# MLP's second layer: where in the first outer product VectorE begins the operand sums of the second one

## The chip, the cores and the metric

One core of a Trainium2 chip runs one program. The time is the device time of one execution in microseconds (us); before the change it is 2250.13 us, the median of three runs (2246.69, 2250.13, 2252.49). The core has five engines that run side by side and meet in semaphores: TensorE (PE for matmuls, PEld for loads of weights), VectorE (DVE), ScalarE (ACT), GpSimd (POOL) and SyncE (SP, which here issues most DMAs).

## The reference

One transformer block on x of 2 x 2048 x 512, all in float32. A condition vector gives shifts, scales and gates:

```python
mod = silu(condition) @ Wada + bada
sh_a, sc_a, gt_a, sh_m, sc_m, gt_m = split(mod, 6, axis=1)
xm = layernorm(x, g1, be1) * (1 + sc_a) + sh_a
x = x + gt_a * attention(xm, Wqkv, Wproj, bproj)     # 16 heads, causal
xm = layernorm(x, g2, be2) * (1 + sc_m) + sh_m
h = gelu(xm @ W1 + b1)                               # 512 -> 2048
x = x + gt_m * (h @ W2 + b2)                         # 2048 -> 512
```

The change lies in `h @ W2`.

## The kernel before

The kernel runs its stages one after the other: modulation, normalised and transposed x, queries, keys and values, attention with its projection (to about 1518 us), and then the MLP in four blocks (`m` = 0 to 3) of 1024 tokens each.

**Products of seven.** Large matrix products are split in two along each side and made with seven block products instead of eight, by Winograd's form of Strassen's method: products named A11, S1, S2, S4, S3, A12, A22, whose operands are blocks of the tokens, or sums and differences of such blocks, against blocks or sums of blocks of the weights. The MLP does this at two levels: seven **outer products**, each made of seven **inner products**. The sums for the weights are made early and kept in DRAM; the sums for the tokens are made by VectorE and GpSimd as the work runs.

**The first layer** of a block (`pair_of_sets`, L2205, for blocks 1 to 3; `first_pair` and `pair`, with single-level weights from the start, for block 0) leaves the hidden values h in eight tiles, gelu included. In the last of its steps for blocks 1 to 3 the gelu of four h tiles isn't issued there but put in the list `ends` (four ScalarE activations), which the second layer works off. For block 0 `ends` stays empty.

**The second layer** of a block is `tail` (L2353). It runs the outer products in the order A11, S1, A12, S2, S3, A22, S4. Each is one call of `outer` (L2284), which has `seven` (L1739) make seven inner products, each of four matmuls (four blocks of 128 of the inner side; a record counts eight, as float32 goes in two passes) of 128 x 256 into a PSUM bank. The inner order is A11, S1, S2, S4, S3, A12, A22, called products 1 to 7 here, or k = 0 to 6 in the code. The banks: products 1, 3, 5 and 7 go to bank ps_a, 2 and 4 to ps_b, 6 to ps_c. Products 3, 4, 5 and 7 add onto what their bank holds, after what it held has been copied out. That is a **drain**: `first` (L2322) behind products 1, 2, 3 and `last` (L2330) behind 4, 5, 6, 7. Where a drain adds (`combine`, L1734) it is on VectorE, where it only copies (L2325, L2335) on ScalarE. In the outer products A11 and S1 the drains behind products 1, 2, 3 and 7 are ScalarE copies, those behind 4, 5 and 6 VectorE additions; in A12, S2, S3, A22 all are VectorE's. Behind S2 and S3 stands one larger VectorE addition of 128 x 1024 each, between results in y.

**The sums.** An outer product needs differences of blocks of h: four for its inner products S1, S2, S3, A22 (`inner_sum`, L1924), and where its own operand is a difference (S1's T1, S2's T2, S3's T3, A22's T4), four pieces of that first. All are `difference` (L1637), of 128 x 1024, on VectorE but for a few early ones on GpSimd. They stand in one list `todo` in a fixed order:

```
A11: 1 | T1(0,0) T1(0,1) | S1: 1 | A11: 2 3 4 | T1(1,0) T1(1,1) | S1: 2 3 4 | A12: 1-4 |
T2 x4 | T1 done | S2: 1-4 | T3 x4 | S3: 1-4 | T4 x4 | A22: 1-4 | S4: 1-4
```

Sum 1 of an outer product is read by its inner product S1, sum 2 by S2, sum 3 by S3, sum 4 by A22. T1(1,1) is also an operand of S1's second sum. "T1 done" issues nothing and gives T1's buffers back. `pop` (L1934) takes the first item of the list and issues it, if a buffer is free (`sums`, a queue of tiles: the buffer given back first is taken first). `need` (L1944) pops until a given sum is issued; `outer` calls it ahead of each inner product for what that reads (and ahead of S1 for sum 2, ahead of S2 for sum 4). In blocks 1 to 3 the last step of the first layer has popped the list's first four items, and then calls for A11: 2, 3, 4.

**The order of the work.** `act` (L209) and `mm` (L205) keep instructions in the order in which the program calls them, engine by engine. So what `then(k)` (L2377) of `tail` issues behind inner product k stands on VectorE's queue behind that product's drain and ahead of the next product's. It issues, in this order: a gate on ScalarE where one is due; one item of `ends`, if there is any, but in A11 only from k = 4 on; one `hid.pop()`, under the condition that the change edits; and `among`, the normalisation and transposes (ps_xt, L215) of the next block's tokens behind k = 3 and 6 of the first four outer products, and its token sums in the last one. The transposes stand on TensorE between outer products. A weight tile's next load (`next_weights`, L1686) is issued behind the inner products S4 and A22.

GpSimd meanwhile adds products of the first layer onto h (L2228), ahead of the gelus in `ends`.

Of the kernel before, what the change touches and what calls it, by code (L numbers as in the profile page):

```python
# [27 lines left out]
def dit_block_kernel(  # L28
# [862 lines left out]
    S1, S2, A11, S4, A12, A22, S3 = range(7)  # L891
# [708 lines left out]
    with ExitStack() as mlp:  # L1600
# [132 lines left out]
        def combine(dst, x, y):  # L1733
            act(nc.vector.tensor_tensor(dst, x, y, ALU.add))  # L1734
# [609 lines left out]
        def gated(m, y, half, i, tok=slice(0, MT)):  # L2344
            b, k = m * 2 * MT // T, half * HK + i
            act(
                nc.scalar.activation(
                    y[:, i, tok], y[:, i, tok], AF.Identity,
                    bias=gbias[:, k, b : b + 1], scale=gb[:, k, b : b + 1],
                )  # L2350
            )

        def tail(m, hid, among, each):  # L2353

            u, c22, c11, c12 = Y
            later = []

            def gate(y, half):
                later.extend(lambda i=i: gated(m, y, half, i) for i in range(2))

            for n, dst, base in (
                (A11, u, None),
                (S1, c22, None),
                (A12, c11, u),  # L2370
                (S2, u, u),
                (S3, u, u),
                (A22, u, u),
                (S4, c12, c12),
            ):

                def then(k):  # L2377
                    if k in (1, 3) and later:
                        later.pop(0)()
                    if hid.ends and (n != A11 or k >= 4):  # L2380
                        hid.ends.pop(0)()
                    if n != A11 or k > 1 or not hid.ends:
                        hid.pop()
                    among(n, k)

                hid.outer(n, dst, base, then, each if n == S4 else None)
                if n == A12:
                    gate(c11, 0)
                elif n == S2:
                    combine(c12, u, c22)  # L2390
                elif n == S3:
                    combine(c22, c22, u)
                    gate(c22, 1)
                elif n == A22:
                    gate(u, 1)
                elif n == S4 and not each:
                    gate(c12, 0)
            for f in later:
                f()
# [31 lines left out]
        for m in range(NM):  # L2431
            hid = Hidden()
# [4 lines left out]
            for p in range(HF // 2):  # L2437

                def among(ph, r):
                    if p == HF // 2 - 1 and not ready:  # L2440
                        if (ph or r == 3) and len(hid.made) < 4:
                            hid.pop()
                    elif p == HF // 2 - 1:
                        if (ph, r) in ((1, 3), (2, 0), (2, 2), (2, 4)):
                            hid.pop()
                    if ready and p < 2 and ph and r in (1, 4):
                        rows_out(m - 1, p, res, [(0, C)], True, (2 * ph - 2 + r // 4,))
# [89 lines left out]
```

## Time and profile before

| | us |
|---|---|
| median of three runs | 2250.13 |
| lowest, highest | 2246.69, 2252.49 |
| profiled execution, its own time | 2247.25 |
| its span, first to last instruction | 2245.5 |
| TensorE busy | 2197.9 (98% of the span) |
| VectorE busy | 1578.2 (70%) |
| ScalarE busy | 1038.3 (46%) |
| GpSimd busy | 1456.7 (65%) |
| granted TensorE clock, mean | 0.997 |
| tails of blocks 1, 2, 3 begin at | 1782.89, 1963.99, 2144.98 |

How to read it: a row of a timeline has the start in us, the duration, the engine, the line of the kernel, the operation, what is written and read (buffer numbers left out), the shapes and the count of instructions that were merged; in brackets stands the idle time of the engine just before, and who ended it. A row of the waits has the waiting engine, tile and line, what it waited for, and the total, the number and the longest of such waits. Matmul ends are modelled, so distances between starts say more than durations. L207 is the helper of all matmuls, L1734 of all VectorE additions (`combine`), L1637 of the sums of blocks; the tile tells them apart: `sum` is a token sum, `y` and `c` are drains of the second layer, `ps_a`, `ps_b`, `ps_c` its banks.

### The profile page before, as it was taken

What the parts mean: (1) busy time and instruction counts of PE and PEld (TensorE: products, weight loads), DVE (VectorE), ACT (ScalarE), POOL (GpSimd) and SP (SyncE); (2) the same over time, 40 slices, a digit from 0 to 9 for tenths busy, and PEclk for the clock granted to TensorE, in tenths of its full rate; (3) what the DMA queues carried; (4) which work ended last, traced back from release to release, by engine and by line L of the source; (5) the groups of instructions that cost most, each with busy time, mean ns of one, the idle gap of its engine ahead of it and who ended that gap; (6) DMA issues with size and microseconds to landing.
All of it is one profiled execution on the core that took longest, in us unless ns stands there. A gap on an engine that the chain in (4) does not pass through costs nothing.

```text
span 2245.5 us, 34306 instructions
## 1 busy us (share of the span) xinstructions
PE 2197.9 (98%) x12273; PEld 1473.3 (66%) x12273; DVE 1578.2 (70%) x3373; ACT 1038.3 (46%) x2132; POOL 1456.7 (65%) x903
## 2 busy tenths in 40 slices
PE   7999999999999999999999999999999999999998
PEld 5787555555543588755555555345788888888887
DVE  4678767777757657777677766665687687687586
ACT  4434555655564243365655556614323523532520
POOL 4254988998983795299989898447416715625540
PEclk9999999999999999999999999999999999999999
DMA  8887142231324899532324113367655555554553
GB/s 280 249 276 191 44 91 67 62 86 48 108 96 139 261 299 314 156 80 71 77 69 102 48 49 131 106 232 260 209 173 207 173 160 169 202 169 157 195 161 107
DMA packets 166628, 340.99 MB, mean 152 GB/s; under 512 B 17217, under 2 KB 49517, under 8 KB 164665
## 3 DMA queue, kind: packets, MB, share of 16 engines
q1 hardware_dynamic: 158080, 302.05, 44.3%
q0 software_dynamic: 8000, 36.21, 4.3%
q8 instruction: 97, 1.59, 0.3%
q14 instruction: 75, 0.61, 0.1%
q10 hardware_dynamic: 376, 0.55, 0.1%
HBM read 246.46 MB, written 100.14 MB: 154 GB/s over the span
## 4 chain that ended last, share of the span: by engine, by line
PE 86%; DVE 6%; POOL 3%; DMA 2%; ACT 1%; issue 1%; SPq 0%; ACTq 0%; DVEq 0%; POOLq 0%
PE ps_a L207 22%; PE st L207 19%; PE ps_b L207 13%; PE o L207 10%; PE s L207 9%; PE ps_o L207 4%; PE ps_c L207 3%; PE sm L207 3%; DVE sum L1637 2%; DVE junk L503 1%; POOL ee L700 1%; PE ps_xt L215 1%; ACT e L675 1%; DVE mx L509 1%; PE ps_o L215 1%
## 5 line engine op out<-in xcount | busy, mean ns | idle before, releaser
L675 ACT ACTIVATE e<-st 128x512 f32<-128x512 f32 (+1 forms) x1152 | 574.9, 578 | 362.4 <-PE st L207 315.6
L509 DVE TENSOR_REDUCE mx<-s 128x1 f32<-128x512 f32 x576 | 381.7, 686 | 193.4 <-PE s L207 192.3
L700 POOL TENSOR_TENSOR ee<-ee,e 128x2048 f32<-128x2048 f32 x106 | 485.8, 4583 | 10.3 <-ACT e L675 4.3
L207 PE MATMUL st<-qst,kst 128*128 128x512 f32 (+3 forms) x1280 | 408.6, 386 | 0.0
L207 PE MATMUL s<-kst,qst 128*128 128x512 f32 (+3 forms) x1046 | 380.6, 395 | 5.7 <-DVE mx L509 3.7
L207 PE MATMUL ps_a<-sum,w 128*128 128x256 f32 (+1 forms) x1304 | 340.2, 395 | 8.3 <-DVE y L1734 7.7
L207 PE MATMUL o<-e,vv 128*32 128x512 f32 (+3 forms) x2560 | 293.2, 537 | 0.3
L207 PEld LDWEIGHTS st<-qst,kst 128*128 128x128 f32 x1280 | 228.5, 188 | 97.7 <-issue 66.0
L207 PEld LDWEIGHTS ps_a<-sum,w 128*128 128x128 f32 x1304 | 249.2, 193 | 51.5 <-DVE y L1734 8.9
L503 DVE CUSTOM_DVE_ANT_0 junk<-s,causal 128x128 bf16<-128x128 f32 (+3 forms) x470 | 220.7, 470 | 60.9 <-PE s L207 47.1
L207 PEld LDWEIGHTS s<-kst,qst 128*128 128x128 f32 x1046 | 194.8, 188 | 70.7 <-DVE mx L509 17.0
L700 POOL TENSOR_TENSOR ee<-e 128x2048 f32<-128x2048 f32 x42 | 192.5, 4584 | 42.7 <-ACT e L675 41.8
L207 PE MATMUL ps_b<-sum,w 128*128 128x256 f32 (+1 forms) x744 | 186.5, 381 | 0.0
L2228 POOL TENSOR_TENSOR h<-h,h 128x512 f32<-128x512 f32 x96 | 119.3, 1271 | 69.8 <-DVE h L1734 69.8
L207 PEld LDWEIGHTS <-sel 32*128 32x128 bf16 x1152 | 29.5, 91 | 197.0 <-issue 195.3
L207 PEld LDWEIGHTS ps_b<-sum,w 128*128 128x128 f32 x744 | 140.6, 190 | 21.8 <-issue 2.6
L509 DVE TENSOR_REDUCE mx<-st 128x1 f32<-128x512 f32 x192 | 131.1, 683 | 0.5
L1799 POOL TENSOR_TENSOR sum<-xm 128x256 f32<-128x256 f32 x22 | 23.2, 1053 | 162.6 <-PE ps_a L207 162.6
L687 POOL TENSOR_SCALAR_AFFINE_SELECT e<-e 128x512 f32<-128x512 f32 x128 | 83.2, 668 | 67.5 <-ACT e L675 67.4
L207 PEld LDWEIGHTS o<-e,vv 128*32 128x32 f32 x2560 | 59.1, 108 | 92.2 <-issue 73.4
L207 PE MATMUL st<-fold,sel 32*128 32x512 bf16 (+1 forms) x1152 | 117.5, 372 | 1.3
L1071 POOL TENSOR_TENSOR lo<-lo,hi 128x512 fp32r<-128x512 f32 x32 | 40.7, 1275 | 105.4 <-ACT hi L1069 103.5
(263 smaller groups left out, 3573.2 us busy)
## 6 DMA issues: line engine op xcount, KB each, us to landing
w<-w1x SPq DMA_DIRECT2D x42, 896.0 KB
qst<-q SPq DMA_DIRECT2D x128, 256.0 KB
kst<-k SPq DMA_DIRECT2D x128, 256.0 KB
w<-w2d SPq DMA_DIRECT2D x28, 1024.0 KB
w<-w2d SPq DMA_DIRECT2D x28, 768.0 KB
q<-hi SPq DMA_DIRECT2D x32, 256.0 KB
q<-lo SPq DMA_DIRECT2D x32, 256.0 KB
k<-hi SPq DMA_DIRECT2D x32, 256.0 KB
```

The lines of the kernel that those rows point to most:

```text
L207: return tc.keep_in_program_order(nc.tensor.matmul(*args, **kw))
L215: return tc.keep_in_program_order(nc.tensor.transpose(dst, src, ident[:n, :n]))
L503: nc.vector.tensor_tensor_reduce(junk[:, :w], x, causal[:, QB - w :], 1.0, MASKED, ALU.add, ALU.max, m,)
L509: self.vector(nc.vector.tensor_reduce(m, x, axis=AX.X, op=ALU.max))
L675: act(nc.scalar.activation(e4[:, h, :w], sts[h][:, :w], AF.Exp))
L687: nc.gpsimd.affine_select(d, d, pattern=[[0, HC], [1, P]], compare_op=ALU.is_ge, fill=0.0, base=0, channel_multiplier=-1,)
L700: act(nc.gpsimd.tensor_tensor(dst, x, y, ALU.add))
L1071: engine.tensor_tensor(lo, d, hi.bitcast(F32), ALU.subtract)
L1637: act(engine.tensor_tensor(dst, x, y, ALU.subtract))
L1799: act(engine.tensor_tensor(dst, u, v, ALU.subtract))
L2228: act(engine.tensor_tensor(d[j], d[j], x[j], ALU.add))
```

## The change

One number in the condition under which `then` pops a sum. In A11 of a block with a filled list `ends` (blocks 1, 2, 3), the pops behind k = 2 and k = 3 go; those behind k = 4, 5 and 6 stay. The list is worked off in the same order, so from T1(1,0) on each pop of it stands two inner products later.

```diff
                 def then(k):
                     if k in (1, 3) and later:
                         later.pop(0)()
                     if hid.ends and (n != A11 or k >= 4):
                         hid.ends.pop(0)()
-                    if n != A11 or k > 1 or not hid.ends:
+                    if n != A11 or k >= 4 or not hid.ends:
                         hid.pop()
                     among(n, k)
```

The order of VectorE's instructions in A11 and the start of S1 (block 1; drains named by their bank):

```
before: A11 2, A11 3, A11 4, T1(1,0), drain ps_b, T1(1,1), drain ps_a, S1 2, drain ps_c, S1 3, S1 4, A12 1, A12 2, A12 3, drain ps_b, A12 4
after:  A11 2, A11 3, A11 4, drain ps_b, drain ps_a, T1(1,0), drain ps_c, T1(1,1), S1 2, S1 3, S1 4, A12 1, drain ps_b, A12 2
```

In A22 the order after is: first drain, A22 2, second drain, A22 3, A22 4, third drain, S4 1; before it was: first drain, A22 4, second drain, S4 1, third drain, S4 2. TensorE, ScalarE and GpSimd have the same operations in the same order; which of the buffers of `sums` they use differs.

## The prediction

> **What bounds the kernel now.** I read the page's first part, then the waits of TensorE alone from 1500 us on (the MLP), then the timelines of TensorE and VectorE around each wait found there, and last the table of stretches for the clock.
>
> ```profile
> PE 2197.9 (98%) x12273; PEld 1473.3 (66%) x12273; DVE 1578.2 (70%) x3373; ACT 1038.3 (46%) x2132; POOL 1456.7 (65%) x903
> ```
>
> TensorE is the bound: 98% busy. A change that moves only VectorE work is worth what TensorE waits for VectorE, no more. The waits of TensorE from 1500 us to the end (total, times, longest):
>
> ```profile
> PE ps_a L207 <- DVE y L1734: 7.7, 3, 2.6
> PE ps_o L215 <- ACT y L2347: 1.5, 1, 1.5
> ...
> PE ps_a L207 <- DVE c L1734: 0.6, 3, 0.2
> ```
>
> The first row is three waits of about 2.6 us for a drain of bank ps_a into y. They stand in the first outer product (A11) of the tails of blocks 1, 2 and 3. The first block's tail has no such wait; its list `ends` is empty, so the edited condition is true there before and after, and nothing changes in it. Here is the second tail on TensorE:
>
> ```profile
> 1789.80 1.89 PE L207 MATMUL ps_a<-sum,w 128*128 128x256 f32 x8
> 1791.53 1.89 PE L207 MATMUL ps_c<-h,w 128*128 128x256 f32 x8
> 1796.00 3.55 PE L207 MATMUL ps_a<-sum,w 128*128 128x256 f32 x8 [2.58 <-DVE y L1734]
> 1799.38 1.04 PE L215 MATMUL ps_xt<-ident,xn 128*128 128x128 f32 x8
> 1800.26 1.89 PE L207 MATMUL ps_a<-sum,w 128*128 128x256 f32 x8
> ```
>
> The rows are inner products 5, 6, 7 of A11, the transposes, and product 1 of the next outer product (S1). Products start 1.73 us apart (1789.80 to 1791.53), transposes take 0.88. Product 7 could start at 1791.53 + 1.73 = 1793.26 and starts at 1796.00: **2.74 us**. It then takes 1799.38 - 1796.00 = 3.38 instead of 1.73: **1.65 us** more. VectorE at that time:
>
> ```profile
> 1785.61 3.37 DVE L1637 TENSOR_TENSOR sum<-h,h 128x1024 f32<-128x1024 f32 x1
> 1788.90 2.30 DVE L1637 TENSOR_TENSOR sum<-h,sum 128x1024 f32<-128x1024 f32 x1
> 1791.12 2.29 DVE L1637 TENSOR_TENSOR sum<-h,h 128x1024 f32<-128x1024 f32 x1
> 1793.33 0.41 DVE L1734 TENSOR_TENSOR y<-c,ps_b 128x256 f32<-128x256 f32 x1
> 1793.67 1.95 DVE L1637 TENSOR_TENSOR sum<-h,h 128x1024 f32<-128x1024 f32 x1
> 1795.54 0.41 DVE L1734 TENSOR_TENSOR y<-c,ps_a 128x256 f32<-128x256 f32 x1
> 1795.87 1.95 DVE L1637 TENSOR_TENSOR sum<-sum,sum 128x1024 f32<-128x1024 f32 x1
> 1797.74 0.41 DVE L1734 TENSOR_TENSOR y<-c,ps_c 128x256 f32<-128x256 f32 x1
> 1798.08 2.35 DVE L1637 TENSOR_TENSOR sum<-sum,sum 128x1024 f32<-128x1024 f32 x2
> ...
> 1851.78 1.22 DVE L1637 TENSOR_TENSOR sum<-h,h 128x1024 f32<-128x1024 f32 x1
> 1852.91 1.75 DVE L1734 TENSOR_TENSOR y<-y,y 128x1024 f32<-128x1024 f32 x1
> 1854.58 0.41 DVE L1734 TENSOR_TENSOR c<-y,ps_a 128x256 f32<-128x256 f32 x1
> 1854.91 1.21 DVE L1637 TENSOR_TENSOR sum<-h,sum 128x1024 f32<-128x1024 f32 x1
> ```
>
> Rows 1 and 2 are the last two of three sums that A11 itself needs; rows 3 and 5 (1791.12, 1793.67) are T1(1,0) and T1(1,1), for the second outer product. The drain of product 5 (1795.54) ends at 1795.95 and product 7 starts at 1796.00. Product 5 had been ready at 1789.80 + 1.89 = 1791.69: the drain was late because two T1 sums stood before it.
>
> Why product 7 is slow is seen in the table of stretches (columns: the stretch, its length, busy time and instructions of PE, PEld, DVE, ACT, POOL, then the granted clock of TensorE, the DMA share, GB/s):
>
> ```profile
> 1793.30:1796.00 2.70, 0.12 (x1) 0.00 (x1) 2.70 (x5) 0.00 (x0) 2.70 (x2) 0.96 0.98 370
> 1796.00:1799.40 3.40, 3.40 (x9) 2.70 (x10) 3.40 (x4) 0.00 (x0) 0.74 (x1) 0.53 0.05 20
> 1799.40:1802.80 3.40, 3.40 (x21) 3.12 (x20) 3.30 (x3) 3.21 (x8) 0.00 (x0) 1.00 0.48 133
> 1977.10:1980.40 3.30, 3.30 (x9) 2.66 (x10) 3.30 (x4) 0.00 (x0) 0.72 (x1) 0.55 0.03 10
> 2158.10:2161.40 3.30, 3.30 (x9) 2.72 (x10) 3.30 (x4) 0.00 (x0) 0.72 (x1) 0.56 0.00 0
> ```
>
> After each wait the clock is 0.53, 0.55, 0.56 for some 3.3 us; after the first of them it is seen back at 1.00. That loses 3.40 x 0.47 = 1.60 in the second tail (1.65 by the starts), 3.30 x 0.45 = 1.49 in the third and 3.30 x 0.44 = 1.45 in the last.
>
> **The change, part by part.** No instruction is added or removed on any engine. Only `hid.pop()` of A11 behind products 3 and 4 goes, in three tails: every VectorE sum from T1(1,0) on stands two places later among the drains, and their buffers rotate accordingly. No DMA and no POOL instruction is moved past another.
>
> *Saved, at A11's product 7.* Behind the sum that ends at 1791.20 now stand two drains: product 4's (ps_b, ready long before), done by about 1791.5, then product 5's, which waits for 1791.69, starts near 1791.73 and ends by 1792.14. Product 7 can go at 1793.26 with 1.1 us to spare. The wait goes whole, 2.74 us in each tail (three alike by the waits row), 8.2 in all. With no idle time, I take it that the clock stays 1.00: 1.65 + 1.49 + 1.45 = 4.6. **Saved 12.8 us**.
>
> *What is late next: S1's product 3.* It needs S1's second sum, which needs T1(1,1). S1 now starts at 1793.26 + 1.73 + 0.88 = 1795.87, so product 3 is due 3.46 later, at 1799.33. GpSimd slows the sums for as long as its own additions last:
>
> ```profile
> 1787.86 8.88 POOL L2228 TENSOR_TENSOR h<-h,y 128x512 f32<-128x512 f32 x4
> ```
>
> They end at 1796.74. VectorE: T1(1,0) from 1792.07 at a pitch of 2.21 (1788.90 to 1791.12) to 1794.28; product 6's drain, 0.34; T1(1,1) at most 2.21 more, to 1796.83; the S1 sum, now free of GpSimd, 1.22, to 1798.05 (1798.8 at the 1.95 of its row). It is 0.5 to 1.3 us early; cost nothing. S1's third and fourth sums follow at about 1.2 each (2.35 for two in the row), ready by 1801.2, before products 5 and 7, due 6.9 and 10.4 after 1795.87. Bank ps_c, which S1 takes over for its second product, is drained by 1794.7, before 1797.6. The cover here is these 0.5 us; past it each microsecond of lateness costs one.
>
> *Then.* In S1's later half, A12, S2 and S3 VectorE has one sum and one drain per product, 1.22 + 0.42 = 1.64 under 1.73; the queue has the same slots, each with a sum of two places before. The task "T1 done" issues nothing and takes one pop wherever it falls. Each sum of S2 and S3 still stands ahead of the product that reads it by a product or more: nothing.
>
> *Lost, at A22 (sixth outer product).* Here there was no spare. Slots by the last four VectorE rows above: a sum (1851.78), the large addition into y (1852.91), a drain, a sum (1854.91). Now the slot at 1851.78 holds A22's first sum and that at 1854.91 its second. TensorE before:
>
> ```profile
> 1852.96 1.89 PE L207 MATMUL ps_b<-sum,w 128*128 128x256 f32 x8
> 1855.05 1.99 PE L207 MATMUL ps_a<-sum,w 128*128 128x256 f32 x8 [0.20 <-DVE c L1734]
> ```
>
> Product 2 reads the first sum, done at 1853.00: 0.1 late at most, which the next wait swallows. Product 3 reads the second, done at 1854.91 + 1.21 = 1856.12, so starts at 1856.17 instead of 1855.05: **1.12 us**. Behind it VectorE has to issue A22's third and fourth sums in one place (product 3 calls for the fourth), one 1.13 us pitch more, ahead of product 3's drain; but that drain's data is 1.12 later too, so nothing more comes late. Same in the third tail. In the last one, where the large addition is shorter:
>
> ```profile
> 2213.13 1.89 PE L207 MATMUL ps_a<-sum,w 128*128 128x256 f32 x8
> ```
> ```profile
> 2212.82 1.22 DVE L1637 TENSOR_TENSOR sum<-h,sum 128x1024 f32<-128x1024 f32 x1
> ```
>
> 2212.82 + 1.22 + 0.05 = 2214.09, less 2213.13: 0.96. **Lost 3.2 us** if the clock stays. The idle time there is about 1.4 us. The nearest row for that is the ps_o wait of the list of waits:
>
> ```profile
> 2230.69 0.77 PE L215 MATMUL ps_o<-ident,y 128*128 128x128 f32 x5 [1.52 <-ACT y L2347]
> ```
> ```profile
> 2230.70:2233.00 2.30, 2.30 (x13) 2.06 (x14) 1.29 (x2) 0.00 (x0) 0.00 (x0) 1.00 0.18 67
> ```
>
> 1.52 us idle, and 1.00 after it. Bounds for the clock at A22: nothing, or 1.6 us a tail as after the 2.58 us waits; 1.4 lies by the 1.52 row, so I take nothing.
>
> **Sum**: 12.8 - 3.2 = 9.6 us. The profiled execution took 2247.25 us (span 2245.5): 2237.7. The three runs have their median at 2250.13, 2.9 above it: **2240.5 us**. About 0.3% (6.75 us) is what a measurement of this kernel can tell from no change.
>
> *A rule against it.* The Trainium skill, TensorE: Matmul & The Clock Gate, section "HAM oscillation — how this bites in real kernels", wants idle gaps of more than about 3.4 us before TensorE falls back to half clock. The rows above show 0.53 behind an idle time of 2.58, so the trace does not bear that threshold out. If the clock there is low for a reason other than the wait, 1.6 us a tail stay: the third rival.
>
> **The rivals.**
> 1. *The A22 wait costs clock too* (1.4 us idle is enough): 3 x 1.6 = 4.8 back, 4.8 saved, 2245.3. For it: 2.58 is not far off and there is one row at 1.52. Against: that row. Chance 0.12.
> 2. *A22 costs nothing* (its sums come earlier than the slots say): 12.8 saved, 2237.3. Against: VectorE has no idle time in that stretch. 0.07.
> 3. *The low clock stays without the wait*: 8.2 - 3.2 = 5.0 saved, 2245.1. Against: 1.00 wherever TensorE runs through. 0.05.
> 4. *Slower: the wait moves to S1's product 3.* If the three sums T1(1,0), T1(1,1) and S1's second each take the longest of their kind, 3.37 (the row at 1785.61, beside a larger GpSimd operation): 1792.07 + 3.29 + 0.34 + 3.29 + 3.37 = 1802.4 against 1799.33, 3.1 idle, 1.6 of clock behind it, 1.1 at A22, less 4.3 saved: +1.5 a tail, 2254.6; with the clock lost at A22 too, +9.3, 2259.4. It decides from 1799.33 + 4.3 - 1.1 - 1.6 = 1800.9 on. Against: GpSimd's additions end at 1796.74. 0.07.
> 5. *It doesn't do what it says*: product 5's drain is held by something other than the sums. Against: VectorE runs without a gap from 1788.90 to it. 0.03, 2250.
>
> **How the numbers follow.** The forecast has 0.66. It lies 2.9 us beyond the bound of 6.75; the runs of before lie up to 3.4 from their median, so I give 0.06 of it to "within". Faster: 0.60 + 0.07 = 0.67. Within: 0.06 + 0.12 + 0.05 + 0.03, and half of rival 4: 0.29. Slower: 0.04. The range takes in the forecast and rivals 1, 2 and 3, 2237.3 to 2245.3, and about a microsecond of scatter: 2236 to 2246.
>
> **What would show it.** Right: the 7.7 us row of TensorE waiting for DVE y is gone; no stretch near 0.5 of the clock in the MLP; S1's first product starts 5 products and 0.88 us after A11's third; a new row of TensorE waiting for a sum (L1637), three times, 1.2 to 1.4 us, before A22's third product, with the clock 1.00 behind it. Wrong: a wait before S1's third product, or a low clock at A22. If both are absent and the gain is not near 9.6, one of the lengths above does not hold.

## The result, and the profile after

The changed kernel takes 2239.77 us in the median of five runs (2239.39 to 2241.53), beside 2246.96 for five runs of the kernel before (2245.70 to 2252.49). The ratio is 0.9963, with a 95% interval of 0.9948 to 0.9978: faster by 8.3 us, between 4.9 and 11.7. The two medians themselves lie 7.2 apart. The forecast was 2240.5, a ratio of 0.9957, 9.6 us less. The profiled execution took 2239.77 us, its span is 2238.1.

The same lines as before, now of the changed kernel. First the page's part 1, then TensorE's waits from 1500 us on:

```profile
PE 2195.8 (98%) x12273; PEld 1470.5 (66%) x12273; DVE 1581.7 (71%) x3373; ACT 1038.3 (46%) x2132; POOL 1456.9 (65%) x903
```
```profile
PE ps_a L207 <- DVE sum L1637: 2.9, 3, 1.1
PE ps_o L215 <- ACT y L2347: 1.5, 1, 1.5
PE ps_o L215 <- DVE xr L1734: 1.1, 3, 0.5
PE ps_a L207 <- DVE c L1734: 0.2, 1, 0.2
```

The three waits of 2.6 us for a drain into y are gone; three waits of up to 1.1 us for a sum have come. The counts of instructions are the same. In the busy shares nothing is to be seen of either: a wait of 8 us in 2240 is below a per cent.

TensorE in the tail of block 1, products 5, 6 and 7 of A11, the transposes, and the first three products of S1:

```profile
1791.98 1.89 PE L207 MATMUL ps_a<-sum,w 128*128 128x256 f32 x8
1793.71 1.89 PE L207 MATMUL ps_c<-h,w 128*128 128x256 f32 x8
1795.44 1.89 PE L207 MATMUL ps_a<-sum,w 128*128 128x256 f32 x8
1797.16 1.04 PE L215 MATMUL ps_xt<-ident,xn 128*128 128x128 f32 x8
1798.04 1.89 PE L207 MATMUL ps_a<-sum,w 128*128 128x256 f32 x8
1799.77 1.89 PE L207 MATMUL ps_b<-sum,w 128*128 128x256 f32 x8
1801.49 1.89 PE L207 MATMUL ps_a<-sum,w 128*128 128x256 f32 x8
```

The products start 1.73 us apart, and the transposes take 0.88. VectorE beside it:

```profile
1791.08 2.29 DVE L1637 TENSOR_TENSOR sum<-h,sum 128x1024 f32<-128x1024 f32 x1
1793.30 0.41 DVE L1734 TENSOR_TENSOR y<-c,ps_b 128x256 f32<-128x256 f32 x1
1793.91 0.42 DVE L1734 TENSOR_TENSOR y<-c,ps_a 128x256 f32<-128x256 f32 x1 [0.20 <-PE ps_a L207]
1794.25 1.34 DVE L1637 TENSOR_TENSOR sum<-h,h 128x1024 f32<-128x1024 f32 x1
1795.64 0.42 DVE L1734 TENSOR_TENSOR y<-c,ps_c 128x256 f32<-128x256 f32 x1
1795.98 1.83 DVE L1637 TENSOR_TENSOR sum<-h,h 128x1024 f32<-128x1024 f32 x1
1797.91 4.38 DVE L1637 TENSOR_TENSOR sum<-sum,sum 128x1024 f32<-128x1024 f32 x3
```

Both drains now stand ahead of the T1 sums; the second even waits 0.20 us for TensorE, so VectorE is ahead here and no longer behind. The granted clock there is 1.00 (columns as in the prediction; it is the third from the right):

```profile
1795.40:1798.80 3.40, 3.40 (x21) 3.04 (x21) 3.25 (x4) 1.44 (x4) 3.40 (x2) 1.00 0.75 281
1854.00:1857.40 3.40, 3.40 (x16) 3.01 (x17) 3.40 (x5) 0.00 (x0) 0.00 (x0) 1.00 0.00 0
```

The second of these rows lies behind the new wait, at A22's third product. That wait on TensorE, and the sum it waits for on VectorE:

```profile
1849.01 1.89 PE L207 MATMUL ps_a<-h,w 128*128 128x256 f32 x8
1850.83 1.99 PE L207 MATMUL ps_b<-sum,w 128*128 128x256 f32 x8
1853.96 1.99 PE L207 MATMUL ps_a<-sum,w 128*128 128x256 f32 x8 [1.14 <-DVE sum L1637]
```
```profile
1850.69 1.75 DVE L1734 TENSOR_TENSOR y<-y,y 128x1024 f32<-128x1024 f32 x1
1852.36 0.41 DVE L1734 TENSOR_TENSOR c<-y,ps_a 128x256 f32<-128x256 f32 x1
1852.69 1.21 DVE L1637 TENSOR_TENSOR sum<-h,sum 128x1024 f32<-128x1024 f32 x1
```

The best measure in one execution is the length of a tail, from A11's first matmul to S4's first, since what comes before the MLP moves it little or not at all. Of the kernel before: 80.90, 80.79, 76.79 us in blocks 1, 2, 3 (starts 1782.89 to 1863.79, 1963.99 to 2044.78, 2144.98 to 2221.77). Of the changed one: 77.61, 77.62, 73.58 (1785.08 to 1862.69, 1962.90 to 2040.52, 2140.73 to 2214.31). That is 3.29 + 3.17 + 3.21 = **9.67 us** shorter. The spans differ by 7.4 only, because the first of these tails started 2.19 us later in the second execution; the MLP's first matmul was at 1514.41 in the one and 1516.59 in the other. In all the executions profiled here it lies between 1513.8 and 1519.3, and the three of the unchanged kernel alone span 1513.82 to 1516.77. What moves that part was not looked into.

### The profile page after: what moved, and what is told of

Read it like the earlier page. It is cut to its first block, busy times and chain, and to the rows that moved or that the text cites. A ratio compares the mean times of both kernels' runs of the same rounds, so it can differ in the third digit from the quotient of the medians.

```text
span 2238.1 us, 34303 instructions
## 1 busy us (share of the span) xinstructions
PE 2195.8 (98%) x12273; PEld 1470.5 (66%) x12273; DVE 1581.7 (71%) x3373; ACT 1038.3 (46%) x2132; POOL 1456.9 (65%) x903
## 4 chain that ended last, share of the span: by engine, by line
PE 88%; DVE 5%; POOL 2%; DMA 2%; ACT 1%; issue 1%; SPq 0%; DVEq 0%; ACTq 0%; POOLq 0%
PE ps_a L207 23%; PE st L207 18%; PE ps_b L207 14%; PE o L207 10%; PE s L207 9%; PE ps_o L207 4%; PE ps_c L207 4%; PE sm L207 4%; DVE junk L503 1%; POOL ee L700 1%; PE ps_xt L215 1%; ACT e L675 1%; DVE mx L509 1%; PE ps_o L215 1%; DMA x<-in_x_dram 1%
## 5 line engine op out<-in xcount | busy, mean ns | idle before, releaser
L207 PE MATMUL ps_a<-sum,w 128*128 128x256 f32 (+1 forms) x1304 | 335.6, 391 | 3.1 <-DVE sum L1637 2.9
```

What stands on the lines that cost most here:

```text
L207: return tc.keep_in_program_order(nc.tensor.matmul(*args, **kw))
```

## The experiments

Two theories stood against each other. **Theory**: TensorE waited at A11's product 7 for a drain that two T1 sums delayed, and lost clock by that wait; the change takes both and pays at A22, where the list is now two places late and VectorE has no spare time. **Rivals**: the clock is low there for another reason, any wait costs clock, the wait at A22 comes from something else, or it only moves to S1.

**1. The changed kernel again** (the file as it is).

> The changed kernel once more, timed beside the one before. Theory (TensorE's wait at A11's product 7 and the low clock behind it are gone, a wait of 1.1 us at A22's product 3 has come): from A11's first matmul to S4's first the tails of blocks 1, 2, 3 take 77.6, 77.6, 73.6 us as in the first profile of it (80.9, 80.8, 76.8 before), and the whole time is 9.7 us below before, ratio 0.9957. Rival (only the 7.2 us between the two medians is real, something outside the tails gives 2 us back): the stretch up to the first tail is 2 us longer again and the ratio is 0.9967.

Median 2240.26 against 2247.26, ratio 0.9963 (0.9951 to 0.9974). Tails 77.61, 77.62, 73.58 (from 1787.77, 1965.59, 2143.42). The tails repeat to 0.01 us. The ratio is nearer to the rival's 0.9967 than to 0.9957 by a little, and its interval holds both: the time of the whole kernel can't tell them apart, the tails can. The first tail starts later again, as the rival had it (1787.77, the latest of all), but in experiments 3 and 9, which do the same work before it, it starts at 1782.49 and 1783.13: that part scatters by itself.

**2. The sums one place earlier.**

```diff
-                    if n != A11 or k >= 4 or not hid.ends:
+                    if n != A11 or k >= 3 or not hid.ends:
```

> The sums begin behind the fourth inner product (k >= 3): one T1 sum stands between the drains of products 4 and 5. Theory: product 7 of A11 waits for that drain by the part of one sum that reaches past 1.73 us after product 6, 0.5 to 0.9 us, without a low clock (idle well under 2.6), and A22 has its second sum in time, so its product 3 waits the 0.2 us of before. A tail is 3.4 to 3.8 us shorter than before (77.1 to 77.5 in block 1), about the changed kernel's time: 10 to 11 us below before. Rival (any idle time of TensorE costs clock): 1.5 us more per tail, clock near 0.55 behind the wait, 6 us below before. Rival (the A22 wait comes with any shift): 1.1 us stay at A22, 7 us below before.

Median 2238.10, ratio 0.9956 (0.9945 to 0.9968). Tails 77.13, 77.14, 73.15: 11.06 us shorter than before, 1.39 less than the changed kernel's. TensorE's waits for VectorE at the inner products:

```profile
PE ps_a L207 <- DVE y L1734: 1.1, 3, 0.4
PE ps_a L207 <- DVE c L1734: 0.6, 3, 0.2
```

One T1 sum between the drains costs 0.4 us, two cost 2.6: the first fits nearly into the time that product 6 takes. The wait is a little under the 0.5 to 0.9 us expected, and the granted clock is 1.00 around all three. Shifted by one place, A22 has its second sum in time, and the wait there is the old one for a drain c. The rival by which any shift brings A22's wait falls, as does the one by which any idle time costs clock.

**3. The changed kernel, with the two places made good before A22.**

```diff
                     if n != A11 or k >= 4 or not hid.ends:
                         hid.pop()
+                        if m and (n, k) in ((S1, 2), (A12, 3)):
+                            hid.pop()
```

> The changed kernel with two more pops, behind product 3 of S1 and product 4 of A12, where VectorE had idle time, so that the list is back at its old place before A22. Theory: A22's wait for a sum goes (0.2 us for a drain stays), A11 keeps its gain: 76.6, 76.5, 72.5 us in the three tails, 12.8 us below before and 3.2 below the changed kernel. Rival (A22's wait is set by the large addition into y, not by which sum stands where): no gain over the changed kernel, 9.6 below before. Rival (the extra sums delay drains in S1 and A12 in turn): new waits of TensorE for y or c there.

Median 2236.95, ratio 0.9952 (0.9938 to 0.9966), the lowest of all, though its interval overlaps with that of the changed kernel, so that the tails have to decide. Tails 76.54, 76.54, 72.58: 12.82 us shorter than before. All that is left of TensorE's waits for VectorE at the inner products:

```profile
PE ps_a L207 <- DVE c L1734: 0.6, 3, 0.2
```

So the gain at A11 alone is 12.8 us, the cost at A22 alone 12.82 - 9.67 = 3.15, and the cost can be avoided, as VectorE has idle time in S1 and A12 (before the change, 3.41 us ahead of S1's drain at 1807.44 and 1.64 ahead of A12's at 1815.15). No new wait came there.

**4. The cost alone**: the kernel before, with the list made two places late behind S1.

```diff
-                    if n != A11 or k > 1 or not hid.ends:
+                    if (n != A11 or k > 1 or not hid.ends) and not (m and n == S1 and k > 4):
                         hid.pop()
```

> The kernel before, A11 as it was, but without the pops behind products 6 and 7 of S1 in blocks 1 to 3: the list is two places late from there on. Theory: A11's wait and its low clock are there in full (2.6 us, 0.55), and A22's product 3 waits 1.1 us for its sum as well: 82.0, 81.9, 77.8 us in the tails, 3.2 us above before, ratio 1.0014. Rival (A22's wait belongs to the earlier start of S1, so to the gain, not to the places): A22 as before, ratio 1.000.

Median 2249.03 against 2247.26, ratio 1.0004 (0.9995 to 1.0012). By the whole time this is a miss: 1.0014 was expected, and the interval holds the rival's 1.000. Tails 82.15, 81.94, 76.44. The waits, though, are those of the theory:

```profile
PE ps_a L207 <- DVE y L1734: 7.8, 3, 2.6
PE ps_a L207 <- DVE sum L1637: 2.9, 3, 1.1
```

A22's wait belongs to the places, not to an earlier start of S1. But the third tail is 0.35 us *shorter* than before instead of 1 us longer, and the clock shows why:

```profile
1797.40:1798.50 1.10, 1.06 (x5) 0.96 (x6) 1.10 (x1) 0.00 (x0) 0.78 (x1) 0.99 0.03 13
1798.50:1801.90 3.40, 3.40 (x14) 2.94 (x13) 3.40 (x5) 1.62 (x4) 0.00 (x0) 0.50 0.17 16
1801.90:1804.00 2.10, 2.10 (x12) 1.84 (x11) 2.00 (x2) 1.45 (x4) 0.00 (x0) 1.00 0.82 274
1979.40:1982.80 3.40, 3.02 (x7) 2.48 (x8) 3.40 (x4) 0.00 (x0) 1.12 (x1) 0.50 0.10 37
2159.40:2161.90 2.50, 0.00 (x0) 0.00 (x0) 2.50 (x4) 0.00 (x0) 2.50 (x2) 1.00 0.49 191
2161.90:2165.40 3.50, 3.46 (x16) 3.07 (x17) 3.50 (x4) 1.00 (x2) 0.78 (x1) 1.00 0.03 4
```

In the first tail the wait ended at 1797.44, TensorE went on at full clock for 1.1 us, and *then* the clock fell, for 3.4 us. In the third the same wait, 2.59 us, had no low clock behind it at all. The clock does not simply follow the wait. This is likely to be why only 0.9 us of the 3.2 expected are seen in the whole time (0.0004 of 2247): the mean granted clock of this kernel's eleven runs is 0.9984, that of the 17 of before 0.9974, and 0.001 of 2247 us is 2.2 us. That is an estimate; only one of the eleven left a trace. The behaviour asked for a theory of its own: the clock is set at the ends of a window of 3.41 us that runs by itself.

**5 and 6. The kernel before, twice more**, for the clock.

> The kernel before, once more, for the clock behind its three waits of 2.6 us. Theory (the clock is set at the ends of a free-running window of 3.41 us: low for one window where the window before it held more than some 1.7 to 2.2 us of TensorE idle time, as the ends of the low stretches of the first profile at 1799.2, 2080.1 less 100, 2161.0 stand 53 windows of 3.413 us apart): the ends of all low stretches in this run stand whole windows of 3.413 us apart to within 0.1, and a wait that a window's end cuts near its middle has no low clock behind it. The tails then take 79.3 instead of 80.9 us (block 1). Rival (each idle time of 2.6 us costs 1.5 us of clock): three low stretches, 80.9, 80.8, 76.8 us.

> The kernel before, a third time, for the clock behind its three waits of 2.6 us. Theory of the free-running window: again ends of low stretches that are whole windows of 3.413 us apart, and the loss behind a wait is 0 or up to 1.7 us by where in the window the wait falls; as the tails start 181.0 us apart, 53.03 windows, the three waits of one execution mostly share their lot. Rival: the same loss of 1.5 us behind every wait in every execution.

One run each, 2248.51 and 2246.64 us. In the first of the two, the tails are 79.32, 81.00, 77.03, in the second 80.86, 80.78, 76.77. The stretches of the first:

```profile
1795.80:1798.30 2.50, 0.00 (x0) 0.00 (x0) 2.50 (x4) 0.00 (x0) 2.50 (x2) 1.00 0.88 319
1798.30:1801.80 3.50, 3.45 (x20) 3.11 (x21) 3.50 (x4) 1.42 (x4) 0.79 (x1) 1.00 0.11 33
1978.30:1981.70 3.40, 3.40 (x11) 2.68 (x10) 3.40 (x4) 0.35 (x2) 0.32 (x1) 0.50 0.01 2
2159.20:2162.60 3.40, 3.40 (x8) 2.69 (x9) 3.40 (x4) 0.00 (x0) 0.62 (x1) 0.50 0.00 0
```

The wait of 2.57 us before 1798.35 left the clock at 1.00, and that tail is 1.6 us shorter, as the theory of the window had said (79.3). Cut into slices of 0.25 us, the low stretches end here at 1981.68 and 2162.59, that is 53 windows of 3.413 apart to 0.02; in the first profile at 1799.17, 1980.09 and 2160.99 (53 and 106 windows); in the second repeat at 1798.55, 1979.45, 2160.36 (53 and 106 again); with the cost alone at 1801.89 and 1982.81 (53). Each is 3.41 to 3.42 us long. The rival, the same loss behind each wait, falls.

**7. A longer wait at A22**: the changed kernel without the pop behind S3's last product.

```diff
-                    if n != A11 or k >= 4 or not hid.ends:
+                    if (n != A11 or k >= 4 or not hid.ends) and not (m and n == S3 and k == 6):
                         hid.pop()
```

> The changed kernel without the pop behind product 7 of S3 in blocks 1 to 3, so that the list is three places late in A22. Theory: A22's first sum now stands behind the large addition and the first drain; product 2 waits for it 3.1 us in blocks 1 and 2 and some 2.6 in block 3, product 3 some 0.1 or not at all. Without a low clock the tails are 2.0 us longer than the changed kernel's (79.6, 79.6, about 75.2). By the free-running window an idle time of 3.1 us leaves at least 1.7 us in one window at nearly every phase, so a low stretch comes in most cases, up to 1.7 us more each. Rival (idle time at A22 costs no clock, whatever its length, since the bank drains go on): 79.6, 79.6, 75.2 and a clock of 1.00.

A miss in the size. One run, 2241.38 us. Tails 78.30, 78.30, 74.43, only 0.7 to 0.9 us longer than the changed kernel's, and TensorE waits 2.0 us, not 3.1:

```profile
PE ps_b L207 <- DVE sum L1637: 5.7, 3, 2.0
```
```profile
1849.03 1.72 DVE L1734 TENSOR_TENSOR y<-y,y 128x1024 f32<-128x1024 f32 x1
1850.68 0.41 DVE L1734 TENSOR_TENSOR c<-y,ps_a 128x256 f32<-128x256 f32 x1
1851.01 1.21 DVE L1637 TENSOR_TENSOR sum<-h 128x1024 f32<-128x1024 f32 x1
1852.26 1.23 DVE L1637 TENSOR_TENSOR sum<-h,sum 128x1024 f32<-128x1024 f32 x1
```

The large addition starts behind the last drain at once, since no sum stands ahead of it: 0.66 us after product 1 (1848.37 to 1849.03), in the changed kernel 1.68 (1849.01 to 1850.69). The expectation had left it there. So the first sum is ready 1 us sooner, product 2 waits 2.0 us for it, and product 3 doesn't wait at all. No low stretch came: the clock stayed 1.00 behind the three waits of 2.01, 2.01 and 1.65 us.

No low stretch in the tails shows the window's edges here, but the start and the end of the program do. In these two rows the clock changes within a tenth of a microsecond:

```profile
22.50:22.60 0.10, 0.10 (x2) 0.10 (x1) 0.10 (x1) 0.00 (x0) 0.10 (x1) 0.82 0.95 348
2237.75:2237.85 0.10, 0.00 (x0) 0.00 (x0) 0.00 (x0) 0.00 (x0) 0.00 (x0) 0.68 0.85 328
```

It rises from 0.50 to 1.00 at 22.54 (0.82 is the mean over that tenth) and falls at 2237.79, behind TensorE's last work: 649 windows of 3.4133 lie between. Another edge then lies at 22.54 + 536 x 3.4133 = 1852.07, and the first wait, 1850.27 to 1852.28, has 1.81 us in the window before it. What a wait of 3.1 us would do to the clock, as expected here, wasn't put to the test.

**8. A wait at A11 in another size**: experiment 2 with three VectorE differences added that nothing reads.

```diff
+                    if n == A11 and k == 3 and hid.ends:
+                        c = spare(half_t)
+                        for _ in range(3):
+                            act(nc.vector.tensor_tensor(c, u[:, 0, :half_t], u[:, 1, :half_t], ALU.subtract))
```

> The sums begin behind the fourth inner product, and three small VectorE differences that nothing reads (128x256, added work) stand with the T1 sum ahead of product 5's drain. Theory: the wait at A11's product 7, 0.38 us without them, grows by three times 0.34 to 0.8 us, to 1.4 to 2.8 us. If it is under 1.7 us no window can hold enough idle time and the clock stays 1.00 in all three tails; if it is 1.7 to 2.6, a low stretch comes only where one window holds nearly all of it. Rival (idle length alone decides): all three tails alike.

A miss in the size again. The three take 3.34 us in all, where 1.0 to 2.4 had been expected, and the wait grew to 3.65 us (one run, 2253.24 us). That is longer than a whole window, so this is no test of waits between 1.7 and 2.6 us, as had been meant. Tails 82.08, 82.09, 79.12: the last is 3.0 us shorter than the others where in the changed kernel it is 4.0, so the clock cost 1.1 us more in it, though the wait is as long (3.63 us): the rival by which the length alone decides falls. There is a low stretch from 1799.67 to 1803.09, one from 1980.58 to 1983.99, and in the last tail two windows in a row:

```profile
2158.00:2161.50 3.50, 1.16 (x6) 0.68 (x4) 3.46 (x3) 0.72 (x1) 3.50 (x3) 1.00 0.70 270
2161.50:2164.90 3.40, 2.11 (x5) 1.76 (x6) 3.37 (x6) 0.00 (x0) 0.16 (x1) 0.50 0.00 0
2164.90:2168.30 3.40, 3.40 (x9) 2.69 (x9) 3.40 (x4) 0.99 (x2) 0.00 (x0) 0.50 0.10 9
2168.30:2171.00 2.70, 2.70 (x14) 2.36 (x13) 1.67 (x2) 1.01 (x3) 0.00 (x0) 1.00 0.83 280
```

**9. The sums one place later at A11.**

```diff
-                    if n != A11 or k >= 4 or not hid.ends:
+                    if n != A11 or k >= 5 or not hid.ends:
```

> The sums begin behind the sixth inner product (k >= 5): T1(1,0) now stands behind product 6's drain too, so that S1's second sum comes later, while the list has caught up before S2 and A22 is as in the changed kernel. Theory: in the changed kernel S1's second sum ended about 1.4 us before S1's product 3 could start; here it ends some 0.5 us later, so still nothing waits in S1, and the tails are 77.6, 77.6, 73.6 us as in the changed kernel. Rival (S1 has no spare time, each delay of its sums is one of TensorE): a wait of TensorE for a sum at S1's product 3, 0.3 to 2 us, tails of 78 to 79.5.

One run, 2237.94 us. Tails 77.62, 77.62, 73.69, and the same waits as the changed kernel's (for a sum, 2.9 in three, longest 1.1). S1's second sum is the first of three in this row of VectorE:

```profile
1797.35 3.50 DVE L1637 TENSOR_TENSOR sum<-sum,sum 128x1024 f32<-128x1024 f32 x3
```

With 1.17 for each it ends about 1798.5; product 3 of S1 is due 16.41 after A11's start (1785.08 to 1801.49 in the changed kernel), here 1783.13, so at 1799.54. The sum has still 1 us to spare: S1 has room, and the rival that it has none falls.

## Why the prediction was right, point by point

- *What bounds the kernel*: right. The gain is what TensorE waited for VectorE, with the clock that went with it.
- *A11's product 7*: right. The wait of 2.74 us by the starts is gone whole in all three tails; the drain ends at 1794.33, 1.1 us before product 7 starts at 1795.44, the 1.1 us to spare that had been worked out. Experiment 3 has this part alone, with its clock: 12.82 us, forecast 12.8. Both go by the same execution of before, in which all three waits had a low clock.
- *The clock*: right that it goes with the wait (rival 3 falls: 1.00 in the changed kernel). The prediction counted 1.5 to 1.65 us in each tail, since the one profiled execution showed three. That is so in that execution, but not in each: of the nine such waits of the kernel before in three profiles, eight had a low stretch, and experiment 4 lacks one of three. So this term of the sum, 4.6 us, is the size of one execution and not a fixed one: the repeat with a stretch missing has tails of 237.35 us in all instead of 238.48, 1.1 less, and would have given 3.5 for the term and 8.5 for the gain. That the profile at hand had all three was not certain. The difference works in the direction of the measured ratio (8.3 us against 9.6), but the interval is too wide to lay the difference on it.
- *S1's product 3* (rival 4): right that nothing waits, though two lengths were off. The first T1 sum took 1.34 us, not 2.2, although GpSimd's additions ran beside it (1790.04 to 1798.94); why is open. So S1's second sum began while they still ran, and took 2.1 us instead of the 1.22 of a sum free of them. The two errors nearly cancel; the sum ended near 1800.0 (4.38 us for three from 1797.91, the last two at 1.14 each), 1.5 us ahead of product 3, where 0.5 to 1.3 had been said. Experiment 9 takes half a microsecond of it away without a trace.
- *A22*: right, to the size. By the starts, products 2 and 3 lose 0.09 + 1.40 = 1.49 us (1849.01, 1850.83, 1853.96 at 1.73 each), of which 0.36 was there before: 1.13, forecast 1.12. In the last tail 0.95 (product 1 at 2201.16, product 3 at 2205.57, less twice 1.73), forecast 0.96. The idle times themselves are 1.1 us twice and 0.6 in the last tail, where the prediction had named 1.2 to 1.4 as its sign. Experiment 4 brings the wait without the gain, experiment 3 the gain without the wait.
- *The clock behind A22's wait* (rival 1): right that none is lost; what the prediction had was one row at 1.52 us. The reason is now better known: 0.6 to 1.1 us of idle time is less than the 1.81 us that a window held in experiment 7 without a low clock behind it.
- *Rival 2*, A22 costs nothing: false for this change, but experiment 3 shows that A22 need not cost anything.
- *The rule held against it*: the trace doesn't bear out that it takes 3.4 us of idle time, as said. The Trainium skill, TensorE: Matmul & The Clock Gate, section "What's actually happening", has a window of 3413 ns that runs freely. The traces agree with that, to 0.02 us over 53 and 106 windows.
- *The time itself*: 2240.5 against 2239.77 is closer than the reasoning deserves. The forecast set out from 2250.13, the median of three runs; the five have 2246.96. The two medians lie 7.2 us apart and not 9.6, and the ratio's 8.3 lies between; the interval holds all of them. The tails, 9.67 us in one pair of profiles, are what bears the sum out.

## What to carry to other kernels

On an engine whose work is kept in the order of the program, put what frees the bottleneck's bank ahead of work that only a later stage needs, and then look where the postponed work comes due: the places lost are still lost five outer products later, even where the engine had idle time on the way, because each slot takes only one item off the list. Give them back in the first idle place (experiment 3, 3.15 us), or move by one place if one fits (experiment 2). To judge an effect of 0.1% to 0.4%, compare the lengths of the stages inside the profiles, which repeat to 0.01 us where the clock isn't in play, not the whole times, which vary by 2 us and more.

## What the hardware showed

The granted clock of TensorE is decided at the ends of windows of 3.413 us, not from the start of a wait. The windows run on through the whole execution: over 53 and 106 of them in the tails, and over 649 from 22.54 to 2237.79 us in experiment 7. Whether a wait costs clock depends on how much of it falls into one window. For the waits whose windows are known from the same execution, I worked out the idle time in each window. With the cost alone, the last wait ran from 2159.35 to 2161.94 and an edge lay at 1801.89 + 105 x 3.413 = 2160.3, so 0.9 and 1.6 us in two windows: no low clock. In the first repeat of the kernel before, 1795.78 to 1798.35 with an edge at 1797.36: 1.6 and 1.0, none. With the added differences, 1794.58 to 1798.23 with edges at 1796.26 and 1799.67: 1.68 in the first window and the clock stayed 1.00, 1.97 in the second and it fell at its end, 1.4 us after TensorE had gone on. In experiment 7, 1.81 us and none. In all other cases 2.05 to 3.35 us in one window came before a low stretch. So the bound lies between 1.81 and 1.97 us here, a little over half a window (the ends of matmuls are modelled, so not to the hundredth); the low clock is 0.50 and lasts for a whole window, once for two, when the first of them held 1.3 us of idle time itself (experiment 8). A wait of less than half a window was never followed by a low clock here.

As the tails of the kernel before start 181.0 us apart, close to 53 windows (180.9), the three waits of one execution fall nearly into the same place of their windows: they lose clock together, or one at the edge is left out. In experiment 4 they start 182.35 and 182.15 apart, so the third wait falls 2.7 us later in its window than the first, and that one had no low clock.
